# Two convolutions in a transformed form and mixer attention in groups of four heads, in an eight-image stack on one core

## The chip, the core and the metric

The kernel runs on one core of a Trainium2 chip. Five engines work side by side, each with its own queue in order: TensorE (PE; its weight loads are listed as PEld), VectorE (DVE), ScalarE (ACT), GpSimd (POOL) and SyncE (SP), which here issues most DMAs. The metric is device time in microseconds, the median of the runs.

## The reference

Input `x` is 8 images of 256 channels on 32 x 32 pixels, in fp32. Four layers follow, each adding to `x` what it makes of its group norm (`_gn`, 32 groups). Cut to what matters here:

```
x = x + attention(gn(x))       # 8 heads of 64, l2-normed q and k, scale 10, 1024 tokens
x = x + conv3x3(gn(x), scaling_factors * quant_weights) + bias
x = x + conv3x3(gn(x), kernel) + bias
x = x + mixer(gn(x))           # per-token norm, 4 selective scans of 1024 steps, gates,
                               # depthwise and pointwise convolutions, 8-head attention
                               # with heads of 32 over 1024 tokens, gelu, 3x3 depthwise, projection
```

Both convolutions have 256 channels in and out, padding 1. The attention of the mixer is

```
att = softmax(q @ k.transpose(0, 1, 3, 2) * (1.0 / hd ** 0.5), axis=-1)     # hd = 32, 8 heads
o = (att @ v).transpose(0, 2, 1, 3).reshape(B, N, Cc)
```

## The kernel before, in words

A channel tile is 128 channels on the 128 partitions, so an image is two tiles of 1024 pixels. Each image goes through the stages A (`front_attention`), O (`front_out`), C (`front_convs`), N and S (`scan_layers`, `scan_steps`), B (`back_layers`, with `mixer_attention`) and E (`back_out`, `back_end`). The engine calls are not issued as they stand: `Plan` records them, and `arrange` orders them for all eight images together, engine by engine, with costs, buffer rooms and due marks (`PACE`) that are written in the file. So stages of different images lie beside each other, in an order that is fixed when the kernel is built. All recorded operations carry one line of the file (L238), so instructions are told apart by their tiles.

PSUM has five rooms: `big` (two tiles of 1024 columns, two banks each), and one bank each of `acc`, `cv`, `da` and `y`. An fp32 product is two TensorE records, a weight load and a matmul each.

A convolution (`conv3x3`) writes the normed image into two padded buffers `im` (34 x 34). For each output tile m and image half h it adds 18 products (two input tiles, nine taps), each of 128 weights columns and 512 pixels, in the one bank `cv`; the weights come as chunks `w` by DMA from ACT's queue, three taps each; then one DVE operation adds the bank to `xt`.

In `mixer_attention` a head has 32 rows. A query tile exists twice, `q[0]` and `q[1]`, each with every other head zeroed (`alt`), so that a product over 64 rows holds one head of two. A unit of `attention` is a pair of heads, a half of the queries and one of eight key tiles: two products of 64 rows side by side (rows 0 to 63 and 64 to 127) fill one `big` tile, ACT takes its exponential (`p<-big`), and two products of 128 x 64 side by side add the values into `acc` (32 value columns and 32 columns of ones per head, the latter for the sums). Values are two units behind scores. `front_attention` has the same form with heads of 64 (`big<-q,k`), and DVE adds up its `p`.

A scan step works on 128 x 1024 elements: POOL multiplies (`hs<-du,bc`), ACT makes two decays (`da`), DVE scans twice, POOL multiplies again (`hs<-hs,bc`); two steps are added up by four products of 32 columns side by side in the bank `y`, 32 such y sums per image. It is fed by DMAs (`du`, `dt`, `bc`) on SP's queue.

Of the kernel before, what the change touches and what calls it, by code (L numbers as in the profile page):

```python
# [2 lines left out]

# [8 lines left out]
F32 = mybir.dt.float32  # L12
I32 = mybir.dt.int32
AF = mybir.ActivationFunctionType
ALU = mybir.AluOpType
# [10 lines left out]
TW = 34 * 34  # L26
# [8 lines left out]
STAGGER = {(128, 128): 5, (64, 128): 109, (128, 64): 56, (128, 32): 29, (32, 128): 150}  # L35
# [3 lines left out]
        (1090, 1090, 1090, 1090),  # L39
        (1794, 2079, 2159, 2247),  # L40
        (3309, 3371, 3408, 3447),
        (4080, 4158, 4180, 4325),
        (4886, 4936, 4988, 5063),
        (5486, 5486, 5525, 5567),
        (6054, 6187, 6240, 6330),
        (7000, 7131, 7262, 7440),
    ),
    "B": (
        (3642, 3818, 3933, 4116),
        (4392, 4437, 4642, 4768),  # L50
        (5155, 5196, 5269, 5284),
        (5865, 5879, 5885, 5955),
        (6550, 6707, 6766, 6867),
        (7291, 7976, 8075, 8299),
        (8403, 8480, 8525, 8749),
        (9837, 9880, 9886, 10001),
    ),
    "C": (
        (2076, 2079, 2141, 2145),
        (2646, 2654, 3354, 3704),  # L60
        (3701, 3911, 4065, 4167),
        (4759, 4784, 4869, 5136),
        (5163, 5377, 5466, 5761),
        (5860, 5879, 6054, 6514),
        (6799, 6868, 6880, 6904),
        (7491, 7558, 7582, 7829),
    ),
    "E": (
        (4096, 4096, 4186, 4285),
        (4827, 4899, 5232, 5286),  # L70
        (5329, 5699, 5832, 6106),
        (6092, 6263, 6350, 7109),
        (7060, 7136, 7688, 7737),
        (8379, 8504, 8574, 8868),
        (9303, 9830, 9895, 10037),
        (12374, 12684, 12908, 13007),
    ),
    "F0": (
        (500, 1149, 1149, 1149),
        (-298, -204, 165, 223),  # L80
        (856, 856, 1011, 1234),
        (2412, 2540, 2540, 2545),
        (-8734, -8678, -8368, -8368),
        (2539, 2864, 4457, 4747),
        (1390, 1390, 1513, 1727),
        (4562, 4572, 4578, 4668),
    ),
    "F1": (
        (2106, 2111, 2131, 2179),
        (1796, 1796, 1943, 2563),  # L90
        (3041, 3041, 3062, 3385),
        (4004, 4068, 4068, 4079),
        (1464, 1603, 1608, 1661),
        (2220, 2318, 2708, 2708),
        (6533, 6538, 6538, 6538),
        (6838, 6870, 6870, 6870),
    ),
    "F2": (
        (2557, 2557, 2685, 3068),
        (3542, 3875, 3875, 3945),  # L100
        (4588, 4595, 4629, 4796),
        (5254, 5343, 5412, 5494),
        (5461, 5871, 5969, 5969),
        (6121, 6642, 6800, 6815),
        (5287, 5445, 5473, 5473),
        (8235, 8306, 8489, 8489),
    ),
    "F3": (
        (3180, 3225, 3267, 3267),
        (3890, 3973, 4076, 4076),  # L110
        (4837, 4838, 4839, 4875),
        (5365, 5369, 5608, 5614),
        (6028, 6083, 6190, 6253),
        (6951, 6955, 6958, 7027),
        (7760, 7854, 8086, 8143),
        (4383, 4745, 5335, 5637),
    ),
    "N": (
        (516, 521, 576, 640),
        (1685, 1687, 2171, 2279),  # L120
        (3467, 4308, 4335, 4362),
        (4483, 4935, 5214, 5225),
        (722, 722, 722, 722),
        (5342, 5342, 5750, 5750),
        (6697, 7072, 7477, 7666),
        (8019, 8302, 8375, 8470),
    ),
    "O": (
        (1416, 1416, 1461, 1501),
        (2356, 2398, 2577, 3153),  # L130
        (3472, 3472, 3472, 3767),
        (4390, 4412, 4416, 4632),
        (5158, 5187, 5225, 5247),
        (5567, 5729, 5751, 5753),
        (6353, 6426, 6427, 6427),
        (7469, 7505, 7506, 7745),
    ),
    "S": (
        (-2043, -509, -169, -165),
        (3552, 3950, 4007, 4072),  # L140
        (4424, 4639, 4959, 5095),
        (3087, 3087, 3087, 3599),
        (-925, -925, -925, -920),
        (3181, 3197, 3203, 3218),
        (3306, 3356, 3356, 3362),
        (7486, 8460, 8543, 8559),
    ),
    "Z0": (
        (2489, 2516, 2580, 2586),
        (-3362, -2551, -2535, -2535),  # L150
        (931, 956, 959, 993),
        (5172, 5207, 5244, 5272),
        (5898, 5898, 5898, 5969),
        (5487, 5487, 5633, 6007),
        (4040, 4070, 4451, 4451),
        (4234, 4308, 4510, 4518),
    ),
    "Z1": (
        (2722, 2752, 3010, 3024),
        (3910, 4021, 4027, 4328),  # L160
        (4647, 4710, 4751, 5149),
        (5328, 5336, 5340, 5374),
        (6040, 6055, 6055, 6115),
        (6520, 6662, 6676, 6688),
        (7664, 7763, 7994, 8414),
        (529, 1313, 1832, 1833),
    ),
    "Z2": (
        (2447, 3260, 3700, 3822),
        (4280, 4280, 4288, 4288),  # L170
        (4852, 4940, 4994, 4994),
        (5570, 5570, 5750, 5886),
        (5953, 6085, 6229, 6295),
        (7061, 7127, 7200, 7329),
        (8177, 8177, 8357, 8478),
        (9006, 9173, 9266, 9274),
    ),
# [1972 lines left out]
```

## Time and profile before

| | us |
|---|---|
| median of 3 runs | 5774.64 (5768.99 to 5777.19) |
| profiled run, its own time | 5783.67 |
| span of the profile | 5781.9, granted TensorE clock 0.941 |
| busy: PE, DVE, ACT, POOL | 5224.1, 3673.7, 2694.6, 2610.2 |
| PE on convolutions, 2304 records | 1076.8 |
| PE on mixer scores (`qk`), 2048 records | 583.1 |
| PE on values of both attentions, 4096 records | 1104.5 |
| PE on front scores (`q,k`), 2048 records | 585.2 |
| ACT on exponentials, 1024 | 1037.4 |
| DVE adding convolution banks to `xt`, 32 and 32 | 23.6 and 21.6 |

A busy time is that of one profiled execution. Groups of PE overlap each other a little, as matmuls are pipelined, and the mean of one matmul includes its latency. Idle time before a group is put down to what released it. Where a row counts records, two make one product.

### The profile page before, as it was taken

How to read it: one execution, taken by the hardware profiler on the slowest of the kernel's cores; microseconds unless marked ns; L12 is line 12 of the kernel's file. 1: busy time of each engine (PE TensorE's matmuls, PEld its weight loads, DVE VectorE, ACT ScalarE, POOL GpSimd, SP SyncE). 2: the span in 40 equal slices, each digit the busy share in tenths (PEclk: the TensorE clock that was granted, in tenths of full speed). 3: DMA queues.
4: the chain of work that ended last, by engine and by line, in shares of the span. 5: the costliest groups of instructions: out<-in, count | busy, mean ns of one | idle time of the engine just before them, and what ended most of it. 6: DMA issues, size and time to landing. Idle time of an engine off the chain costs nothing.

```text
span 5781.9 us, 52549 instructions
## 1 busy us (share of the span) xinstructions
PE 5224.1 (90%) x17318; PEld 1811.6 (31%) x17318; DVE 3673.7 (64%) x4517; ACT 2694.6 (47%) x3115; POOL 2610.2 (45%) x1302
## 2 busy tenths in 40 slices
PE   8999789999999989999899999998989988868895
PEld 3333232332333233333323323342233332322333
DVE  4434757666776668646678647866466665677713
ACT  3323334545454544545454554544635436546442
POOL 0000865178601864118533745509650377497500
PEclk9999789999999989999999999999999999879897
DMA  1112433144402433124422433224340354233200
GB/s 52 31 49 82 129 109 106 54 122 124 128 24 80 126 108 94 46 59 136 119 76 66 133 96 110 79 67 134 93 134 17 110 148 114 83 106 106 74 21 32
DMA packets 252411, 516.99 MB, mean 89 GB/s; under 512 B 65112, under 2 KB 131288, under 8 KB 252128
## 3 DMA queue, kind: packets, MB, share of 16 engines
q1 hardware_dynamic: 168032, 402.35, 24.8%
q10 hardware_dynamic: 84096, 111.19, 6.8%
q8 instruction: 139, 2.28, 0.2%
q14 instruction: 144, 1.18, 0.1%
HBM read 448.84 MB, written 56.10 MB: 87 GB/s over the span
## 4 chain that ended last, share of the span: by engine, by line
PE 37%; DVE 12%; DMA 6%; ACT 4%; POOL 3%; issue 3%; SPq 0%; ACTq 0%; DVEq 0%; POOLq 0%
PE big L238 21%; PE acc L238 8%; PE cv L238 6%; DVE hs L238 4%; POOL hs L238 3%; PE y L238 2%; ACT da L238 2%; DVE room L238 2%; DMA dt<-dt_m 1%; DVE u L238 1%; DMA du_m<-a 1%; DMA w<-in_wc 1%; DVE p L238 1%; DMA dt_m<-dt 1%; ACT p L238 1%
## 5 line engine op out<-in xcount | busy, mean ns | idle before, releaser
L238 POOL TENSOR_TENSOR hs<-du,bc 128x1024 f32<-128x1024 f32 x512 | 1245.7, 2440 | 2529.3 <-DMA du<-du_m 1813.2
L238 ACT ACTIVATE p<-big 128x1024 f32<-128x1024 f32 x1024 | 1037.4, 1020 | 807.9 <-PE big L238 732.4
L238 POOL TENSOR_TENSOR hs<-hs,bc 128x1024 f32<-128x1024 f32 x512 | 1295.3, 2531 | 187.5 <-DVE hs L238 115.6
L238 ACT ACTIVATE da<-dt,a_neg 128x512 f32<-128x512 f32 x1024 | 707.2, 691 | 1135.1 <-DVE hs L238 894.1
L238 PE MATMUL cv<-im,w 128*128 128x512 f32 x2304 | 1076.8, 614 | 54.0 <-ACT im L238 21.0
L238 PE MATMUL acc<-p,v 128*64 128x512 f32 x4096 | 1104.5, 623 | 8.5 <-ACT both L238 3.0
L238 DVE TENSOR_TENSOR_SCAN hs<-da,hs 128x512 f32<-128x512 f32 x512 | 624.5, 1220 | 404.9 <-ACT da L238 268.1
L238 DVE TENSOR_TENSOR_SCAN hs<-da,carry,hs 128x512 f32<-128x512 f32 x512 | 654.9, 1279 | 338.8 <-ACT da L238 269.1
L238 DVE TENSOR_TENSOR p<-p 128x1024 f32<-128x1024 f32 x448 | 600.0, 1340 | 275.9 <-ACT p L238 210.5
L238 PEld LDWEIGHTS cv<-im,w 128*128 128x128 f32 x2304 | 429.8, 194 | 681.8 <-issue 562.8
L238 PE MATMUL big<-qk,qk 64*128 64x512 f32 x2048 | 583.1, 650 | 63.4 <-ACT p L238 37.3
L238 PE MATMUL big<-q,k 64*128 64x512 f32 x2048 | 585.2, 652 | 58.7 <-ACT k L238 20.6
L238 PEld LDWEIGHTS acc<-p,v 128*64 128x64 f32 x4096 | 214.8, 136 | 775.1 <-issue 691.6
L238 PE MATMUL y<-hs,sel 128*32 128x512 f32 x2048 | 338.6, 643 | 85.5 <-POOL hs L238 83.7
L238 PEld LDWEIGHTS big<-qk,qk 64*128 64x128 f32 x2048 | 160.7, 188 | 473.4 <-issue 231.0
L238 PEld LDWEIGHTS big<-q,k 64*128 64x128 f32 x2048 | 160.7, 189 | 466.8 <-issue 256.0
L238 PE MATMUL big<-xn,w 128*128 128x512 f32 x512 | 231.9, 603 | 7.2 <-ACT big L238 3.5
L238 PE MATMUL big<-o,w 128*128 128x512 f32 x384 | 178.7, 608 | 8.2 <-DVE o L238 7.0
L238 DVE SCALAR_TENSOR_TENSOR room<-room,vec,room 128x992 f32<-128x992 f32 (+1 forms) x128 | 160.7, 1255 | 9.7 <-ACT room L238 8.1
L238 DVE SCALAR_TENSOR_TENSOR u<-raw,vec,u 128x1024 f32<-128x1024 f32 x96 | 141.8, 1477 | 31.1 <-ACT u L238 30.2
L238 PE MATMUL big<-xm,w_minw 64*128 64x512 f32 x256 | 137.0, 651 | 18.9 <-DVE room L238 6.5
L238 PEld LDWEIGHTS y<-hs,sel 128*32 128x32 f32 x2048 | 49.2, 110 | 321.5 <-POOL hs L238 187.9
(220 smaller groups left out, 4845.6 us busy)
## 6 DMA issues: line engine op xcount, KB each, us to landing
bc<-bc SPq DMA_DIRECT2D x1024, 128.0 KB
w<-in_wc ACTq DMA_DIRECT2D x384, 192.0 KB
dt<-dt_m SPq DMA_DIRECT2D x512, 128.0 KB
du<-du_m SPq DMA_DIRECT2D x512, 128.0 KB
rs<-inv SPq DMA_DIRECT2D x64, 256.0 KB
dt_m<-dt SPq DMA_DIRECT2D x64, 256.0 KB
du_m<-a SPq DMA_DIRECT2D x64, 256.0 KB
w<-in_wqk ACTq DMA_DIRECT2D x64, 128.0 KB
```

The costliest lines, as they stand in the source:

```text
L238: made = op["call"](*args, **kwargs).ins
```

## The change

It has three parts. **Convolutions.** Two neighbouring pixels of a row are made of four products instead of six: the normed image is split into odd and even columns and turned into four tap images (`taps`: a difference, a sum, a difference and a difference), each 16 columns wide, in halves of 16 rows with their border rows (`transform`, on ACT and DVE). For each output tile and image half, 24 products of 256 pixels (four taps, three rows, two input tiles) go in two turns of 12 through the bank `cv`; `add_products` adds the first turn to `xt` with three DVE operations and the second with one. The weights of the inner taps are half sums and half differences of the three weights of a row; `conv_weights` makes them once, at the start, and writes all to DRAM (stage V). A chunk `w` is now 256 KB, of four matrices.

**Scores.** `q` is no longer zeroed by heads, and four products of 32 rows, one for each head of a tile, fill both `big` tiles; two exponentials follow. **Values.** The four heads of a unit go to two banks, `acc` for two heads and `cv` for the other two, one unit behind the scores. The number of exponentials and of value products is as before.

The planner learns of it: products of 32 rows may be grouped over two tiles, a group may take several buffers at once, PE's writes count as whole banks, and the due marks of all stages and one charge for product shapes (`STAGGER`) are other numbers. The diff, without the due marks, the planner's bookkeeping, and the copying out of values, which stays in kind:

```diff
-STAGGER = {(128, 128): 5, (64, 128): 109, (128, 64): 56, (128, 32): 29, (32, 128): 150}
+STAGGER = {(128, 128): 5, (64, 128): 109, (128, 64): 56, (128, 32): 29, (32, 128): 300}
...
+def whole_banks(r):
+    return r[:3] + (r[3] // HALF * HALF, r[4] // HALF * HALF + HALF - 1)
...
-                if joins and first.tensor.name == out.tensor.name:
+                beside = first.tensor.name == out.tensor.name or rows == 32
+                if joins and beside:
...
+        if op["engine"] == 0:
+            outs = [whole_banks(r) for r in outs]
...
-        src = fc_w if name == "fcw" else I[name]
+        src = made_w.get(name, I[name])
...
+    made_w = {"fcw": fc_w}
+    for name in ("wc1", "wc2"):
+        made_w[name] = wdp.tile([12, P, 4, P], F32, tag=name, name=name)
+    minus_s1 = wp.tile([P, 2], F32, name="minus_s1")
+    vector.tensor_scalar_mul(minus_s1, vec[:, cols["s1"] : cols["s1"] + 2], -1.0)
...
-    images = [wp.tile([P, TW], F32, name="im%d" % t) for t in range(2)]
+    taps = wp.tile([P, 2, 4, 18, 16], F32, name="taps")
...
-    def conv3x3(xt, mv, made, name, bname, evac):
-        im = [t.rearrange("p (h w) -> p h w", w=34) for t in images]
-        group_norm(
-            xt, group_stats(mv, cv_tile), [t[:, 1:33, 1:33] for t in im], image
-        )
-        for m in range(2):
-            scalar.activation(xt[m], xt[m], AF.Identity, bias=col(bname, m))
-        for m in range(2):
-            for h in range(2):
-                ps = cv_tile()
-                n = 0
-                for c in range(2):
-                    for dy in range(3):
-                        w = chunk(name, (m * 2 + c) * 3 + dy)
-                        for dx in range(3):
+    def conv_weights(name):
+        for i in range(6):
+            w = room[0][:, 0 : 6 * P].rearrange("p (c k n) -> p c k n", c=2, k=3)
+            sync.dma_start(out=w, in_=I[name][i])
+            sums = room[1][:, 0 : 4 * P].rearrange("p (c k n) -> p c k n", c=2, k=2)
+            plus, minus = sums[:, :, 0], sums[:, :, 1]
+            vector.tensor_add(plus, w[:, :, 0], w[:, :, 2])
+            vector.tensor_scalar_mul(w[:, :, 1], w[:, :, 1], 0.5)
+            vector.scalar_tensor_tensor(
+                minus, plus, 0.5, w[:, :, 1], ALU.mult, ALU.subtract
+            )
+            vector.scalar_tensor_tensor(
+                plus, plus, 0.5, w[:, :, 1], ALU.mult, ALU.add
+            )
+            inner_w, outer_w = (
+                made_w[name][2 * i + k].rearrange("p (c k) n -> p c k n", c=2)
+                for k in range(2)
+            )
+            sync.dma_start(out=inner_w, in_=sums)
+            for k in range(2):
+                sync.dma_start(out=outer_w[:, :, k], in_=w[:, :, 2 * k])
+    def transform(xt, stats, h):
+        scale, shift = stats
+        rows = slice(0, 17) if h == 0 else slice(16, 32)
+        n = rows.stop - rows.start
+        if h == 0:
+            vector.memset(taps[:, :, :, 0], 0.0)
+        else:
+            vector.tensor_copy(taps[:, :, :, 0], taps[:, :, :, 16])
+            vector.memset(taps[:, :, :, 17], 0.0)
+        for c in range(2):
+            t = taps[:, c, :, 1 : 1 + n]
+            for k, at in ((1, 1), (2, 0)):
+                scalar.activation(
+                    t[:, k],
+                    image(xt[c])[:, rows, at:32:2],
+                    AF.Identity,
+                    bias=shift[:, c : c + 1],
+                    scale=scale[:, c : c + 1],
+                )
+            odd, even = t[:, 1], t[:, 2]
+            vector.tensor_sub(t[:, 0, :, 1:16], odd[:, :, 0:15], odd[:, :, 1:16])
+            vector.tensor_sub(t[:, 3, :, 0:15], even[:, :, 1:16], even[:, :, 0:15])
+            for k, src, at in ((0, odd, 0), (3, even, 15)):
+                scalar.mul(t[:, k, :, at], src[:, :, at], -1.0)
+            vector.tensor_add(odd, odd, even)
+            vector.scalar_tensor_tensor(even, even, -2.0, odd, ALU.mult, ALU.add)
+    def add_products(x, ps, inner_taps, scales):
+        pixels = x.rearrange("p (h w k) -> p k h w", w=16, k=2)
+        products = ps.rearrange("p (k h w) -> p k h w", k=2, w=16)
+        def add(to, part, scale, minus=False):
+            if scale is not None:
+                vector.scalar_tensor_tensor(to, part, scale, to, ALU.mult, ALU.add)
+            else:
+                (vector.tensor_sub if minus else vector.tensor_add)(to, to, part)
+        plus, minus = scales or (None, None)
+        if inner_taps:
+            shape = [P, 2, 16, 16]
+            add(pixels, products[:, 0].unsqueeze(1).to_broadcast(shape), plus)
+            add(pixels[:, 0], products[:, 1], plus)
+            add(pixels[:, 1], products[:, 1], minus, True)
+        else:
+            add(pixels, products, plus)
+    def conv3x3(xt, mv, made, name, bname, scales, finish):
+        stats = group_stats(mv, cv_tile)
+        for h in range(2):
+            half = HALVES[h]
+            transform(xt, stats, h)
+            for m in range(2):
+                scalar.activation(
+                    xt[m][:, half], xt[m][:, half], AF.Identity, bias=col(bname, m)
+                )
+            for m in range(2):
+                for part, ks in enumerate(((1, 2), (0, 3))):
+                    ps = cv_tile()
+                    w = [chunk(name, (m * 3 + dy) * 2 + part) for dy in range(3)]
+                    for i, k in enumerate(ks):
+                        for n in range(6):
+                            dy, c = divmod(n, 2)
                             tensor.matmul(
-                                image(ps),
-                                w[:, dx],
-                                im[c][:, 16 * h + dy : 16 * h + dy + 16, dx : dx + 32],
+                                ps[:, i * C : (i + 1) * C].rearrange(
+                                    "p (h w) -> p h w", w=16
+                                ),
+                                w[dy][:, 2 * c + i],
+                                taps[:, c, k, dy : dy + 16],
                                 start=n == 0,
-                                stop=n == 17,
+                                stop=n == 5,
                             )
-                            n += 1
-                evac(m, HALVES[h], ps)
+                    add_products(xt[m][:, half], ps, part == 0, scales(m))
                 if h == 1:
                     channel_stats(made, m, xt[m])
+                finish(m, half)
...
         xt = img.pop("x")
-        def evac_1(m, part, ps):
-            part = xt[m][:, part]
-            vector.scalar_tensor_tensor(
-                part, ps, col("s1", m), part, ALU.mult, ALU.add
-            )
+        def scales(m):
+            return col("s1", m), minus_s1[:, m : m + 1]
         mv = stats_tile()
-        conv3x3(xt, img.pop("mv"), mv, "wc1", "b1", evac_1)
+        conv3x3(xt, img.pop("mv"), mv, "wc1", "b1", scales, lambda m, half: None)
         img["xd"] = xdp.tile([P, 2, N], F32, tag="xd", name="xd")
-        def evac_2(m, part, ps):
-            vector.tensor_add(xt[m][:, part], xt[m][:, part], ps)
-            sync.dma_start(out=img["xd"][:, m, part], in_=xt[m][:, part])
-        conv3x3(xt, mv, mvs[:, img["at"]], "wc2", "b2", evac_2)
+        def finish(m, half):
+            sync.dma_start(out=img["xd"][:, m, half], in_=xt[m][:, half])
+        conv3x3(
+            xt, mv, mvs[:, img["at"]], "wc2", "b2", lambda m: None, finish
+        )
         img["made"] = True
...
                             stop=c == 1,
                         )
                 if at == t:
-                    q = [work("qk3")[:, 0:N] for _ in range(2)]
+                    q = work("qk3")[:, 0:N]
                     vector.tensor_scalar(
-                        q[0], ps, col("ain_b", t), alt[:, 0:1], ALU.add, ALU.mult
-                    )
-                    scalar.activation(
-                        q[1], ps, AF.Identity, bias=alt_b[:, t, 1:2], scale=alt[:, 1:2]
+                        q, ps, col("ain_b", t), 32.0**-0.5, ALU.add, ALU.mult
                     )
                 else:
                     k = work("qk3")[:, 0:N]
...
-        attention([lambda i=i: pair(i) for i in (0, 1, 4, 5)], False)
+        def scores(u):
+            if u["t"] not in qk:
+                q_and_k(u["t"])
+            (q, k), kt = qk[u["t"]], u["kt"]
+            s = [big_tile() for _ in range(2)]
+            for e in range(4):
+                rows = slice(e * 32, e * 32 + 32)
+                tensor.matmul(
+                    s[e // 2][:, HALVES[e % 2]],
+                    k[rows, kt * P : (kt + 1) * P],
+                    q[rows, HALVES[u["h"]]],
+                    start=True,
+                    stop=True,
+                )
+            u["p"] = [work("p")[:, 0:N] for _ in range(2)]
+            for p, ps in zip(u["p"], s):
+                scalar.activation(p, ps, AF.Exp)
+        def values(u):
+            t, h, kt = u["t"], u["h"], u["kt"]
+            if kt == 0:
+                accs[t, h] = acc_tile(), cv_tile()
+            for at, acc in enumerate(accs[t, h]):
+                for e in range(2):
+                    tensor.matmul(
+                        acc[e * 64 : e * 64 + 64],
+                        v[:, kt, 4 * t + 2 * at + e],
+                        u["p"][at][:, HALVES[e]],
+                        start=kt == 0,
+                        stop=kt == NKT - 1,
+                    )
+            if kt == NKT - 1:
+                take(t, h)
...
+        sums, accs = {}, {}
+        units = [
+            {"t": t, "h": h, "kt": kt}
+            for t in range(2)
+            for h in range(2)
+            for kt in range(NKT)
+        ]
+        for n in range(len(units) + 1):
+            for stage, at in ((scores, n), (values, n - 1)):
+                if 0 <= at < len(units):
+                    stage(units[at])
...
+    with plan.part("V", 0):
+        conv_weights("wc1")
+        conv_weights("wc2")
...
-        return c(w.transpose(0, 2, 4, 3, 5, 1).reshape(12, P, 3, P))
+        return c(w.transpose(0, 4, 3, 2, 5, 1).reshape(6, P, 2, 3, P))
```

## The prediction

> **What bounds the kernel now.** I read the page first: the shares of the engines and the row of the granted clock.
>
> ```profile
> PE 5224.1 (90%) x17318; PEld 1811.6 (31%) x17318; DVE 3673.7 (64%) x4517; ACT 2694.6 (47%) x3115; POOL 2610.2 (45%) x1302
> ...
> PEclk9999789999999989999999999999999999879897
> ```
>
> TensorE is busy nine tenths of the span; the others have room on average. An average hides stages, so I cut the span where the PE order gives a landmark. The orders of the two kernels show that everything issued on PE before the first y sum of image 6's scan is the same work in both, convolutions apart; that sum starts at 4596 us. Columns: stretch, length, busy time of PE, PEld, DVE, ACT, POOL, granted clock, DMA share, GB/s.
>
> ```profile
> 0.00:4596.00 4596.00, 4257.97 (x14036) 1472.54 (x14036) 2966.88 (x3769) 2147.25 (x2490) 1978.92 (x991) 0.96 0.32 90
> 4596.00:5010.00 414.00, 371.37 (x1257) 128.38 (x1256) 267.23 (x277) 204.56 (x245) 304.78 (x152) 0.94 0.43 119
> 5010.00:5432.00 422.00, 317.44 (x1084) 98.25 (x1084) 322.72 (x281) 218.38 (x260) 325.64 (x160) 0.84 0.39 109
> 5432.00:5782.00 350.00, 277.32 (x947) 112.41 (x946) 116.84 (x191) 124.37 (x120) 0.90 (x1) 0.85 0.08 24
> 2200.00:2300.00 100.00, 99.23 (x325) 31.19 (x325) 85.55 (x104) 48.52 (x59) 49.43 (x26) 1.00 0.30 84
> ```
>
> To 4596 us PE is 93% busy: less PE work is time there. In the third stretch, the last scan, PE is 75% busy and POOL has 326 us of 422: the scan sets the pace. The last is image 7's back half, a chain. The fifth row shows that DVE at 85% does not slow PE.
>
> Next the groups of instructions, shapes apart (count | busy us, mean ns | idle before it and its releasers).
>
> ```profile
> L238 PE MATMUL cv<-im,w 128*128 128x512 f32 x2304 | 1076.8, 614 | 54.0 <-ACT im L238 21.0 <-DMA w<-in_wc 18.6 <-DVE xt L238 14.3
> L238 ACT ACTIVATE p<-big 128x1024 f32<-128x1024 f32 x1024 | 1037.4, 1020 | 807.9 <-PE big L238 732.4 <-PE cv L238 14.1 <-DVE t L238 8.5
> ...
> L238 PE MATMUL big<-qk,qk 64*128 64x512 f32 x2048 | 583.1, 650 | 63.4 <-ACT p L238 37.3 <-DVE a L238 10.4 <-DVE qk L238 10.1
> ```
>
> A product is two records, so 1152 convolution products and 512 pairs of mixer scores. PE waits little for either: 54 and 63 us.
>
> **Convolutions.** 18 products of 512 columns per (m, h) become 24 of 256. The 256-column shape is already there, in the values of the mixer; the timeline has two runs of it.
>
> ```profile
> 1204.05 3.72 PE L238 MATMUL big<-w,x 128*128 128x256 f32 x16
> ...
> 2485.99 7.17 PE L238 MATMUL big<-w,x 128*128 128x256 f32 x32
> ```
>
> (7.17 - 3.72)/16 = 0.216 us a record. Rows of 512 columns (16 records 7.03 us, 8 records 3.60 us) give 0.429, so the shape halves cleanly, and a weight load of 0.19 us still fits under 0.216. By the orders, 1044 of 1152 products lie before the landmark now, and 1476 of 1536 after the change: 2088 x 0.429 = 896 us against 2952 x 0.216 = 638. That is 258 us at full clock, 269 at the 0.96 granted. The Trainium skill (TensorEngine Tiling (Array Packing), Instruction Overhead) speaks against many short products: some 60 cycles are lost on each. Read as an addition at the 2.4 GHz of its page TensorE: Matmul & The Clock Gate, the 864 more records would cost an estimated 22 us and the gain would be 247; the row shows none of it, and the measurement decides.
>
> What convolutions gain in hand-overs: one PSUM bank (cv) now turns 128 times instead of 64, and the tap buffer is filled 32 times instead of 16. Now a turn costs PE 14.3/64 = 0.22 us and a fill 21.0/16 = 1.3; at these prices +14 and +21, so +35 us. Lower bound 0. The upper bound is a turn with nothing on PE to cover it; that is a rival below. In the order most turns have scores, values or y sums between (one run of 42 products has none).
>
> DVE: from 512-column rows (0.738 scaled, 0.676 plain) and 1024-column rows (1.273, 1.209) an operation is 0.14 to 0.20 us plus 1.04 ns a column. A filled half image is four operations of about 0.44 us on each channel tile: 64 x 1.74 = 111 us. An evacuation pair is 2.4 or 2.2 us, 64 of them 147 us, against 45 now. With small copies 10 and the weight transform 20, DVE gets 243 us more, 3917 in all, 73% of 5400. I cost it at nothing, since the last windows row above runs PE at 99% beside 85% DVE; if that cover fails it is part of the third rival. ACT: identities on 272 columns instead of 1024, about +70 us, less 19 for the second scaled copy of q that goes: under 1% of the span, cost 0. DMA: chunks of 256 instead of 192 KB, 25 MB more; weights cost PE 18.6 us now and twelve short products need 768 KB in 5.2 us, so 0 to 25 us; I take 0, since runs are spread among attention.
>
> The weight transform puts 48 DMAs on SP's queue and 48 DVE operations into the first 280 us, ahead of sums, few, inv and rs of image 0's attention. DVE is half idle there and the first convolution starts near 280 us; twelve rounds of load, four operations and stores at some 8 us (estimate) are 96 us. Cost 0, at most 30 if the stores hold up the normalisers.
>
> **Mixer scores.** Now a pair of 64-row products, an exp, a pair of values:
>
> ```profile
> 4100.78 1.13 PE L238 MATMUL big<-qk,qk 64*128 64x512 f32 x4
> ...
> 4101.84 1.08 PE L238 MATMUL acc<-p,v 128*64 128x512 f32 x4
> ...
> 4102.02 1.03 ACT L238 ACTIVATE p<-big 128x1024 f32<-128x1024 f32 x1 [1.04 <-PE big L238]
> 4102.85 0.30 PEld L238 LDWEIGHTS big<-qk,qk 64*128 64x128 f32 x4 [0.81 <-issue]
> ```
>
> One round takes 4102.85 - 4100.78 = 2.07 us, PE without a gap, ACT idle half of it. Two rounds, four heads: 4.14. After it: one quad of 32-row products, two exps, two pairs of values. No row here has 32-row products. Nearest: the y sums, four 32-column products side by side, 1.06 us; and the pair, whose four loads take 0.30 (0.19 + 3 x 0.037), so eight take 0.45 and the quad 1.06 + 0.15 = 1.21. Other end: two pairs one after the other, 2.12, or four single products, 3.45. I take 1.21, because both packed forms in the trace do overlap.
>
> PE then needs 1.21 + 2 x 0.99 = 3.19. But a quad fills both big buffers, so the next quad waits for both exps: 1.24 from quad to first exp (4102.02 - 4100.78), 2 x 1.03, and some 0.15 back (that first exp starts 0.11 after its pair's 1.13), 3.45 us. That chain, not PE, sets the round: 0.69 saved instead of 0.95. In ACT's order 49 of 256 quads have another operation between their exps, nearly always a decay (0.69 us); 36 are in images 0 to 5. Other ACT work has the 1.24 us. Before the landmark: 160 quads x 0.69 less 36 x 0.69 = 85 us, 89 at clock 0.96. Queued behind a quad waiting on PE are values and y sums, and so the scan; a y sum stands in every third round and fits its gap. The skill's PSUM Bottleneck section (same Tiling page) warns that packed products move the limit to the engine that empties PSUM. The trace has that engine 0.26 us per round behind PE, which is the chain just priced; were ACT always late by a decay, the round would be 4.1 and this term about 0.
>
> **Sum**, from the span of 5781.9:
> - to the landmark 4596 - 269 - 89 + 35 = 4273;
> - scan of image 6: 414 loses nearly all its convolution and a third of its scores, but POOL alone has 305 and the last scan, with PE free, took 422: 395;
> - scan of image 7, already paced by the scan: 415;
> - image 7's back half: 350 - 32 x 0.69 = 328.
>
> Together 5411, with 1.8 us around the span 5413. The profiled run (5783.7) is 9 above the median (5774.6), so 5404; I say 5400, 6.5% less.
>
> **Rivals.**
> 1. The covers hold better: quads at PE's 3.19 with decays in the gaps (-70), turns hidden (-35), two scans nearer to POOL's 320 (-45): 5250. For it: PE at 97 to 99% in busy windows. Against: both big buffers are taken by one quad.
> 2. The change does not do what it says: 32-row products run two abreast. The round is 2.12 + 1.98 = 4.1 as now, so 89 + 22 come back: 5510. Four in a row, 5.43 a round: 160 x 1.29/0.96 + 89 before the landmark and 63 in the back half, 5770. For: no such row. Against: y's quads at 1.06.
> 3. DVE is late now and then: a quarter of the hand-overs below stand uncovered: 5520.
> 4. Slower: the one cv bank and the one tap buffer. A turn without cover is an evacuation of 1.7, a scan of 1.2 ahead of it on DVE and 0.3 of signalling, 3.2 us; 128 are 410. A fill is four ACT and eight DVE operations, about 6 us; 32 are 190. All uncovered: 5400 - 35 + 600 = 5965; at three quarters 5815. It decides from 68%, where 5775 is reached. For: one bank, in-order queues. Against: 0.22 us a turn today.
>
> **How the numbers follow.** Forecast 5400 (own range 5310 to 5480) 0.55; rival 1 0.20; rival 2 0.09; rival 3 0.11; rival 4 0.05. The range 5220 to 5540 takes in rivals 1 to 3, and leaves out part of rival 1, four-in-a-row quads and rival 4. The three runs spread by 0.14%; about 0.2% is what can be told from no change. Faster 0.94, same 0.01, slower 0.05.
>
> **What would show it.** Right: cv records near 0.22 us apart and PE's cv group near 700 us; a qk quad near 1.2 us; ACT's two exps back to back and PE idle about 0.3 us a round, put down to ACT p; idle before cv below 120 us; DVE about 3900 us; the two last scans still about 400 us each. Wrong: quads over 2 us (rival 2), cv idle of 200 us or more released by DVE xt or ACT taps (rivals 3 and 4), or first y sum of image 6 later than 4400 us.

## The result, and the profile after

The changed kernel takes **5817.3 us** (median of 5 runs) where the kernel before takes 5774.6. The ratio of the two kernels is 1.0077, 95% interval 1.0057 to 1.0098: slower by 0.8%. I had forecast 5400.

First the page of the changed kernel: busy times and their share of the span, then the granted clock in 40 slices.

```profile
PE 4872.9 (84%) x18086; PEld 1946.9 (33%) x18086; DVE 3930.9 (68%) x5060; ACT 2709.1 (47%) x3353; POOL 2611.0 (45%) x1295
...
PEclk9999889888998889989899989989999877888796
```

PE's busy time fell by 351 us, but its idle time rose from 5781.9 - 5224.1 = 558 to 5815.6 - 4872.9 = 943. The second row is why the busy time fell by so little: the mean granted clock went from 0.941 to 0.896. In both traces the clock is granted either whole or half; PE was busy for 467 us at half clock before and for 799 after. Counting these at half, I estimate PE's work at full clock as 4991 us before and 4473 after. So some 518 us of PE work did go; about 167 came back as a lower clock, and 385 as idle time.

The stretches of the prediction, cut at the same landmark (the first y sum of image 6, now at 4613.4). Columns as there: stretch, length, busy PE, PEld, DVE, ACT, POOL, clock, DMA share, GB/s.

```profile
0.00:4613.40 4613.40, 3996.64 (x14908) 1633.42 (x14908) 3222.44 (x4319) 2175.20 (x2729) 1987.66 (x988) 0.92 0.35 99
```

Up to the landmark I had 4273; it is 4613, against 4596 before. Most of the error, 340 of some 404 us, is in this one stretch: PE is 87% busy in it instead of 93%, at a clock of 0.92 instead of 0.96. From the landmark to the end of the last y sum of image 7 it is 875 us where it was 838 and where I had 810. Image 7's back half alone came out as forecast: 328 us, from 5488 to the end.

PE's waits, longest sums first (us, times, longest); first before, then after.

```profile
PE y L238 <- POOL hs L238: 83.7, 37, 5.8
PE big L238 <- ACT p L238: 59.6, 45, 10.1
```

```profile
PE y L251 <- POOL hs L251: 199.2, 82, 12.2
PE acc L251 <- ACT p L251: 133.3, 147, 9.6
PE big L251 <- DVE u L251: 49.1, 12, 12.8
```

PE now comes to a y sum 82 times before POOL has weighed the scan's states, and to the values 147 times before ACT has made the exponentials. Most of both lies where scans run. I added up PE's idle time by slices of 100 us: in slices where POOL, which works for the scans, is at least 40% busy it rose from 326 to 642 us, elsewhere from 232 to 300. One pair of such slices, before and then after (columns: slice, length, busy PE, PEld, DVE, ACT, POOL, clock, DMA share, GB/s):

```profile
4700.00:4800.00 100.00, 96.68 (x310) 36.89 (x310) 68.72 (x60) 43.16 (x55) 83.67 (x42) 0.98 0.58 159
```

```profile
4700.00:4800.00 100.00, 55.03 (x144) 17.73 (x144) 71.21 (x57) 31.80 (x40) 70.55 (x35) 0.68 0.33 87
```

PE falls from 97 to 55% and its clock from 0.98 to 0.68, while DVE and POOL, at 71% each, are the busiest and neither is near full. So the busy time of no single engine accounts for that slice.

The pieces themselves are as I sized them. Two runs of convolution products in the timeline (start, us, engine, instruction):

```profile
935.25 5.45 PE L251 MATMUL cv<-taps,w 128*128 128x256 f32 x24
965.41 1.56 PE L251 MATMUL cv<-taps,w 128*128 128x256 f32 x6
```

(5.45 - 1.56)/18 = 0.216 us a record, the value of the sum (the whole group is 762.6 us busy, where I had said near 700). And image 7's mixer, which has no scan beside it:

```profile
5578.62 1.08 PE L251 MATMUL cv<-p,v 128*64 128x512 f32 x4
5578.78 1.94 ACT L251 ACTIVATE p<-big 128x1024 f32<-128x1024 f32 x2 [1.38 <-PE big L251]
5579.86 1.08 PE L251 MATMUL acc<-p,v 128*64 128x512 f32 x4 [0.16 <-ACT p L251]
5580.87 1.14 PE L251 MATMUL big<-qk,qk 32*128 32x512 f32 x8
5581.94 1.08 PE L251 MATMUL cv<-p,v 128*64 128x512 f32 x4
5582.10 1.94 ACT L251 ACTIVATE p<-big 128x1024 f32<-128x1024 f32 x2 [1.38 <-PE big L251]
```

A round is 5582.10 - 5578.78 = 3.32 us, where I had 3.45. The quad takes 5581.94 - 5580.87 = 1.07, where a pair of 64-row products took 1.06 before: four products of 32 rows do run side by side.

### The profile page after: what moved, and what is told of

Read it like the earlier page. It is cut to its first block, busy times and chain, and to the rows that moved or that the text cites. A ratio compares the mean times of both kernels' runs of the same rounds, so it can differ in the third digit from the quotient of the medians.

```text
span 5815.6 us, 55053 instructions
## 1 busy us (share of the span) xinstructions
PE 4872.9 (84%) x18086; PEld 1946.9 (33%) x18086; DVE 3930.9 (68%) x5060; ACT 2709.1 (47%) x3353; POOL 2611.0 (45%) x1295
## 4 chain that ended last, share of the span: by engine, by line
PE 49%; DVE 19%; DMA 10%; ACT 8%; POOL 7%; issue 5%; SPq 1%; ACTq 0%; DVEq 0%; POOLq 0%
PE big L251 27%; PE acc L251 9%; PE cv L251 9%; POOL hs L251 7%; DVE hs L251 6%; ACT p L251 3%; DMA dt_m<-dt 2%; ACT da L251 2%; PE y L251 2%; DMA dt<-dt_m 2%; DVE p L251 2%; SPq L251 1%; DVE u L251 1%; DVE room L251 1%; DMA du<-du_m 1%
## 5 line engine op out<-in xcount | busy, mean ns | idle before, releaser
L251 ACT ACTIVATE p<-big 128x1024 f32<-128x1024 f32 x1024 | 1018.4, 1019 | 670.0 <-PE big L251 582.5
L251 PE MATMUL acc<-p,v 128*64 128x512 f32 x3072 | 854.1, 640 | 141.5 <-ACT p L251 133.3
L251 PE MATMUL cv<-taps,w 128*128 128x256 f32 x3072 | 762.6, 402 | 105.3 <-DVE taps L251 35.4
L251 PEld LDWEIGHTS cv<-taps,w 128*128 128x128 f32 x3072 | 597.7, 200 | 346.8 <-issue 136.6
L251 PE MATMUL y<-hs,sel 128*32 128x512 f32 x2048 | 413.3, 689 | 206.4 <-POOL hs L251 199.2
L251 PEld LDWEIGHTS acc<-p,v 128*64 128x64 f32 x3072 | 164.9, 139 | 744.3 <-issue 373.3
L251 PE MATMUL big<-qk,qk 32*128 32x512 f32 x2048 | 369.1, 697 | 46.2 <-ACT raw L251 14.0
L251 PE MATMUL cv<-p,v 128*64 128x512 f32 x1024 | 288.1, 636 | 2.7 <-DVE xt L251 2.7
L251 PEld LDWEIGHTS big<-qk,qk 32*128 32x128 f32 x2048 | 101.9, 198 | 299.8 <-issue 196.4
L251 POOL COPY carry<-hs 128x2 f32<-128x2 f32 x256 | 107.4, 420 | 169.1 <-DVE hs L251 145.6
```

Of the source, the lines that this page charges most:

```text
L251: made = op["call"](*args, **kwargs).ins
```

## The experiments

Theories after the first look: **A**, the quads lock PE to ACT and the scan; **B**, the convolutions' new work on DVE and their single bank eat the gain; **C**, the order, which the planner makes from costs and due marks, decides, whatever the work is. Times are medians; ratios stand against runs of the kernel before that were made beside each.

### One part alone, a control, and the old marks

The first two kernels are the changed one with one part put back; the third is the program of before under the planner of the change; the fourth is the changed one with the marks of before.

```diff
 # e1: conv3x3, transform, add_products, conv_weights of the change
-        ... (scores and values in units of four heads)
+        attention([lambda i=i: pair(i) for i in (0, 1, 4, 5)], False)
 # e2: units of four heads
-    def conv3x3(xt, mv, made, name, bname, scales, finish):
+    def conv3x3(xt, mv, made, name, bname, evac):
 # e4
-PACE = {"A": ((-805, -722, -708, -698), ...
+PACE = {"A": ((1090, 1090, 1090, 1090), ...
```

> The convolutions of the change alone (four products per two pixels, tap buffer, weight transform), with the mixer attention of before; planner of the change, marks of before. Theory A (the quads lock the mixer to ACT and the scan; the convolutions keep their gain): about 269 - 35 us less than before, 5500 to 5580 us. Theory B (the convolutions' DVE work, which waits on POOL, and the single cv bank eat their gain): 5750 us or more. Theory C (the order of the planner, not the work, makes the difference): anything, but as far from before as the control with the program of before under the same planner is.

> The mixer attention of the change alone (quads of 32-row scores, values in two banks), with the convolutions of before; planner of the change, marks of before. Theory A: no gain or a loss, 5770 to 5950 us, and PE waits for ACT p ahead of acc for 100 us or more. Theory B: the gain that I predicted for the scores, some 110 us, stays: 5640 to 5700 us. Theory C: as far from before as the control.

> Control: the program of before, with its marks, ordered by the planner of the change (which counts a PSUM write as a whole bank, gives out several tiles at once and costs 32-row products at more). Theories A and B: within 0.5% of before, 5746 to 5803 us. Theory C: over 1% from before, so that a comparison of single parts must allow for that much.

> The changed program with the due marks of before (the weight transform keeps its own). Theory C (the new marks are what costs the time): 5400 to 5600 us. Theories A and B (the work itself sets the time): 5800 us or more, the marks of the change fitting it better than those of before.

| | us | ratio to before (95%) |
|---|---|---|
| e1, convolutions alone, marks of before | 6209.5 | 1.0787 (1.0755 to 1.0819) |
| e2, quads alone, marks of before | 6448.5 | 1.1188 (1.1165 to 1.1210) |
| e3, program and marks of before, new planner | 5768.7 | 1.0000 (0.9987 to 1.0012) |
| e4, change with marks of before | 6375.5 | 1.1061 (1.1036 to 1.1085) |

e2 missed every forecast. e1 lies in B's range (5750 or more) and e4 in that of A and B (5800 or more), but both are so far beyond what the change itself costs that this speaks for neither. The planner's edits are neutral for the program of before (e3). A program that is ordered by marks made for another is 8 to 12% slower here, ten times or more what the change costs. So single parts can't be judged in such an order, and A and B stay open here. Each of the three shows the same wait first among PE's (e2, then e4; 341.5 us in e1):

```profile
PE y L242 <- POOL hs L242: 486.6, 164, 11.6
```

```profile
PE y L241 <- POOL hs L241: 509.6, 171, 10.9
```

The marks say when the work of each stage and image is due, and so where it stands in the orders of the engines. In these three orders PE meets the scan's y sums too early: this wait was 83.7 us before.

### Less work in the same order

To test the work without the order, I left products out after the order had been made: every engine keeps its list, and only the named instructions are missing. These programs, and e10 and e12 below, leave out a part of the result and serve to price work alone. In e7 one memset of the tap buffer at the start is added.

```diff
-        for n in arrange(self.ops, self.rooms):
+        for n in (k for k in arrange(self.ops, self.rooms) if not self.ops[k].get("left_out")):
...
 # e5, in the kernel before, after each product
+                            plan.ops[-1]["left_out"] = plan.recording and dx == 1
 # e6, in the changed kernel, after each product
+                            plan.ops[-1]["left_out"] = plan.recording and n in (1, 3)
 # e7: in transform, each of the four DVE operations after the two activations
```

> The kernel before, every engine's instructions in the same order, but the convolutions' products with the middle column of taps (dx = 1) left out: 384 of 1152 products, 768 records x 0.429 = 330 us of PE work, as much as the change takes off the convolutions, and nothing added. Step on test: 'to 4596 us PE is 93% busy: less PE work is time there'. If it holds: 0.9 x 330 = 300 us less, 5450 to 5500 us. If it fails (the orders of ACT, DVE and POOL are as long as PE's, and PE only fills their waits with convolutions): under 80 us less, 5690 to 5775 us; PE idle grows by about what its busy time loses, the granted clock falls, and PE's wait for POOL hs ahead of y grows.

> The changed kernel, every engine's instructions in the same order, but a third of the convolutions' products left out (the second channel tile in two of three rows of taps): 512 of 1536 products, 1024 records x 0.216 = 221 us of PE work. If PE's work sets the time after the change: about 190 us less, near 5630 us. If the other engines' orders do: within 60 us of the changed kernel, 5755 to 5820 us.

> The changed kernel, every engine's instructions in the same order, but DVE's four operations that make the transformed taps left out in all fills (256 operations, some 120 us of DVE with their waits on POOL). If DVE's new work, or its turns with POOL, is what delays the scan and with it PE (the cover that I costed at nothing): 100 us or more less, 5715 us or below. If the orders set the pace and DVE has room: within 40 us of the changed kernel, 5775 to 5855 us, a little of either sign.

e5 took 5712.9 us, ratio 0.9900 (0.9884 to 0.9917): 330 us of PE work less, nothing added, and 55 us gained on the runs of before made beside it. The page and PE's first waits of e5:

```profile
PE 4992.5 (87%) x16550; PEld 1680.8 (29%) x16550; DVE 3679.7 (64%) x4517; ACT 2693.3 (47%) x3115; POOL 2608.4 (46%) x1302
...
PE 48%; DVE 21%; DMA 11%; POOL 7%; ACT 7%; issue 6%; SPq 1%; ACTq 0%; DVEq 0%; POOLq 0%
PE big L238 29%; PE acc L238 11%; DVE hs L238 8%; POOL hs L238 6%; PE cv L238 5%; ACT da L238 3%; DMA dt<-dt_m 2%; PE y L238 2%; DMA w<-in_wc 2%; DVE p L238 2%; DVE room L238 2%; DMA dt_m<-dt 2%; DVE u L238 2%; SPq L238 1%; ACT p L238 1%
```

```profile
PE y L238 <- POOL hs L238: 115.3, 60, 6.4
PE big L238 <- ACT p L238: 77.3, 56, 10.1
PE cv L238 <- DVE xt L238: 51.8, 20, 9.1
```

PE's busy time falls by 232 us and its idle time rises from 558 to 724; the clock goes from 0.941 to 0.926. The second part of the page is the chain that ended last: though PE is busy 87% of the span, it holds 48% of the chain, and `cv` only 5%. By this chain, convolutions mostly fill PE's time while other work holds the end.

e6 took 5749.7 us, 68 below the changed kernel's 5817.3, for 221 us of PE work: just beyond the bound of 60 that I had set for orders, and far from 190. e7 took 5768.8 us, 48 below it: between my two cases. 256 DVE operations took 3930.9 - 3783.9 = 147 us, 0.57 each where I had 0.44. Three quarters of them in the changed kernel (count; min, median and max in ns; first and last start in us; shapes):

```profile
L251 DVE TENSOR_TENSOR taps<-taps x192: 376/418/2609, 241.1 to 4633.2; 128x255 f32<-128x255 f32 x64, 128x240 f32<-128x240 f32 x64, 128x272 f32<-128x272 f32 x32, 128x256 f32<-128x256 f32 x32
```

Most take 0.42 us, but some 2.6; POOL's multiplications take 2.4 to 2.5. One place in the timeline of the changed kernel, DVE and POOL alone:

```profile
822.76 0.43 DVE L251 SCALAR_TENSOR_TENSOR taps<-taps 128x272 f32<-128x272 f32 x1
822.94 7.50 POOL L251 TENSOR_TENSOR hs<-du,bc 128x1024 f32<-128x1024 f32 x3 [31.68 <-DMA du<-du_m]
823.11 5.11 DVE L251 TENSOR_TENSOR taps<-taps 128x255 f32<-128x255 f32 x2
828.33 2.41 DVE L251 SCALAR_TENSOR_TENSOR taps<-taps 128x272 f32<-128x272 f32 x1
```

While POOL multiplies three times, three operations on the taps take 2.4 to 2.6 us each. Over the whole trace 34 of the 256 take more than 0.7 us, 72 us together. In each of the 34 a POOL instruction was already running when the operation started, and 32 of them ended 0.26 to 0.30 us after that instruction did; of the 221 that took at most 0.5 us only 18 overlap POOL at all. So these operations wait for POOL. The Trainium skill (SBUF — State Buffer, Who interferes with whom) says that DVE's second pair of SBUF ports is GpSimd's too, under an exclusive lock; the trace agrees with it. Cover that I had priced at nothing cost up to 48 us in this order; it is a part, not the cause.

### Less work in an order made anew

```diff
 # e10 and e12, in the kernel before
                         for dx in range(3):
+                            if dx == 1:
+                                n += 1
+                                continue
 # e8, e9, e11 to e14: other numbers in PACE alone
```

For new marks I varied them step by step and kept what the planner reckoned to end no later; e8 and e9 for about as long as each other, e11 to e14 longer.

> The changed kernel with other due marks: the same instructions, the marks varied step by step and kept wherever the planner's own reckoning ended no later, some hundred thousand steps from the marks of the change. If the order alone holds back what PE was spared: far below both, 5400 to 5600 us. If the new marks only trim an order that is as long in the other engines as in PE: 1 to 2% below the changed kernel, 5700 to 5770 us, and no further below the next run than the changed kernel is from the one before.

> The control to the last run: the kernel before with marks varied in the same way and for as long from its own. If the marks of before were closer to their best than those of the change (the change was only less well ordered): within 0.3% of before, 5750 to 5785 us. If both were as far from it: 1 to 1.5% below, 5690 to 5720 us, and still no slower than the changed kernel with new marks.

> As the second run before these (the kernel before without the convolutions' products of the middle column of taps, 330 us of PE work less), but here the planner never sees those products and makes its order anew, with the marks of before. If less PE work is worth time in any sensible order: at most the 5713 us of the run in the old order. If the marks fit one program's work and no other: slower than before though it does less, 5850 to 6000 us, with PE waiting for POOL hs ahead of y for 200 us or more.

> The changed kernel with marks varied for longer, from those of its first run with new marks (5762 us). If that was still badly ordered: 5720 to 5745 us, 0.4 to 0.8% under the kernel before. If 5762 us was about what this program can do: 5750 to 5770 us. In neither case do I now expect the 5400 us of my forecast.

> The kernel before without the convolutions' products of the middle column of taps (330 us of PE work less; planned without them, as in the run that took 5984 us), with marks varied for this program. Compare with the kernel before with new marks, 5733 us. If an order made for it turns PE work into time: 300 us less than that, near 5430 us. If the other engines' orders are nearly as long as PE's however it is ordered: 60 to 140 us less, 5590 to 5675 us, a fifth to two fifths of the work.

> The convolutions of the change alone, as in the run of 6209 us, with marks varied for this program. If the 6209 us were the order: 5720 to 5800 us, within 1.2% of the kernel before with new marks (5733 us). If the convolutions themselves are slow (DVE's taps, the single bank): 5850 us or more. My own sum would have it 235 us below 5733.

> The mixer attention of the change alone, as in the run of 6448 us, with marks varied for this program. If the 6448 us were the order: 5740 to 5840 us. If the quads themselves are slow beside a scan (both big tiles taken, exps behind decays): 5900 us or more. My own sum would have it 110 us below 5733.

| | us | ratio to before (95%) | PE idle | clock |
|---|---|---|---|---|
| e8, change, new marks | 5761.6 | 0.9987 (0.9969 to 1.0006) | 905 | 0.900 |
| e9, before, new marks | 5733.5 | 0.9944 (0.9925 to 0.9964) | 508 | 0.942 |
| e10, before less a third of the products, marks of before | 5984.3 | 1.0382 (1.0359 to 1.0405) | 904 | 0.898 |
| e11, change, marks varied for longer | 5695.8 | 0.9878 (0.9861 to 0.9894) | 862 | 0.903 |
| e12, as e10, new marks | 5618.6 | 0.9750 (0.9734 to 0.9766) | 646 | 0.926 |
| e13, convolutions alone, new marks | 5760.7 | 0.9984 (0.9972 to 0.9997) | 751 | 0.916 |
| e14, quads alone, new marks | 5729.9 | 0.9948 (0.9930 to 0.9966) | 661 | 0.929 |

(PE idle is the span less PE's busy time of the profiled run; e5 is the run that e10's text means.)

e10 does less than the kernel before and is 219 us slower. Its first wait of PE:

```profile
PE y L238 <- POOL hs L238: 336.9, 119, 10.4
```

It was 83.7 us before. The same products in the old order took 5712.9 (e5), so what made e10 slow is the order. With marks of its own (e12) the same program takes 5618.6, which is 115 below e9, for 330 us of PE work. So an order made for the lighter program turns about a third of the work into time, and less if the longer search for e12's marks gave a part of it; in the old order it was a sixth. In e12 PE holds 55% of the chain:

```profile
PE 4960.9 (88%) x16550; PEld 1674.3 (30%) x16550; DVE 3681.7 (66%) x4517; ACT 2688.8 (48%) x3113; POOL 2600.4 (46%) x1302
...
PE 55%; DVE 18%; DMA 10%; ACT 7%; POOL 5%; issue 4%; SPq 1%; ACTq 0%; DVEq 0%; POOLq 0%
```

e13 and e14 show that the 6209 and 6448 us of e1 and e2 were mostly the order: in orders of their own the parts take 5761 and 5730, e13 within my bounds and e14 a little below them. Neither is clearly better than e9, though their marks were varied for longer, so neither part alone brought what I had summed for it (235 and 110 us below e9).

e12 and e13 together say more. By the estimate used above for the kernels before and after, their PE work at full clock is the same, 4670 and 4680 us; both were ordered anew, and e13 takes 142 us more. What the convolutions of the change add beside their products (251 us of DVE work, hand-overs, larger weight chunks, the weight transform) took back all that the lighter products gained; my sum had it at 35. So theory B holds for the convolutions, as far as two orders can be compared. e7's 48 us for four of DVE's operations, in another order, is the only piece of it that was priced. For the quads, e14's values wait 92.0 us for ACT p, where e9 has 10.7 us of idle time before values in all: that fits theory A, and no run takes the wait away.

e11, the changed kernel, is 121 us faster than with the marks that it came with, below the 5720 that I gave as the lowest, and 1.2% faster than before: the version that beats both. Its page and waits:

```profile
PE 4838.9 (85%) x18086; PEld 1938.7 (34%) x18086; DVE 3920.1 (69%) x5060; ACT 2703.0 (47%) x3353; POOL 2602.6 (46%) x1295
```

```profile
PE y L241 <- POOL hs L241: 167.3, 67, 10.7
PE acc L241 <- ACT p L241: 146.8, 141, 9.9
```

The wait for POOL hs shrank from 199 to 167 us; the wait of values for ACT p did not, and PE still idles 862 us. e9 missed both of its cases: 0.6% better than before, so the marks of before were closer to good ones than those of the change, but not at their best. e8 against e9, varied alike, is 5761.6/5733.5 = 1.005, so the change did not gain in that comparison. e11 against e9 is 5695.8/5733.5 = 0.993, but its marks were varied for longer.

**Open.** A control for e11, the kernel before with marks varied as long, was not run; the gain of the change at equal care of the order lies, by e8, e9 and e11, between a loss of 0.5% and a gain of 0.7%, and a better order may exist for any of them. Which of the other engines holds the rest is not separated either: PE waits for the scan on POOL and for exponentials on ACT in every run. No run here has POOL's or ACT's work taken away.

## Why the prediction was wrong

The step that failed is the one behind every term up to the landmark: **"To 4596 us PE is 93% busy: less PE work is time there."** e5 tests it without the change: 330 us of PE work are worth 55 us, a sixth, where the step gives 300, and e12 at most 115 in an order made for it. The first y sum of image 6 then started at 4613, past the 4400 that I had named as a sign of being wrong. A busy share says what an engine does, not what the end waits for. The page of before had rows against it, which I did not weigh: its chain that ended last.

```profile
PE 37%; DVE 12%; DMA 6%; ACT 4%; POOL 3%; issue 3%; SPq 0%; ACTq 0%; DVEq 0%; POOLq 0%
PE big L238 21%; PE acc L238 8%; PE cv L238 6%; DVE hs L238 4%; POOL hs L238 3%; PE y L238 2%; ACT da L238 2%; DVE room L238 2%; DMA dt<-dt_m 1%; DVE u L238 1%; DMA du_m<-a 1%; DMA w<-in_wc 1%; DVE p L238 1%; DMA dt_m<-dt 1%; ACT p L238 1%
```

The shares add up to 65%, for the chain is followed back only to 1940 us. PE holds 37 of the 65, and `cv` 6 of the 65, about a tenth, where convolutions are a fifth of PE's busy time (1076.8 of 5224.1). If the first third is like the rest, a third of the convolutions is then worth 0.06/0.65/3 = 3% of the span, an estimate of some 178 us, if nothing else came late next; 55 were measured. So the chain warns, and it still priced the work too high.

Two rows of the changed kernel for what follows: a wait of PE up to the landmark (us, times, longest), and the group of convolution products (busy us, mean ns | idle before).

```profile
PE acc L251 <- ACT p L251: 94.0, 85, 9.6
```

```profile
L251 PE MATMUL cv<-taps,w 128*128 128x256 f32 x3072 | 762.6, 402 | 105.3 <-DVE taps L251 35.4
```

By the terms of the sum:
- **Convolutions, 269.** The size was right (0.216 us a record). Its worth was not: 55 us for as much work in the old order (e5), at most 115 in an order of its own (e12), and nothing once the work that comes with it is there (e13).
- **Scores, 89.** The quad (1.07 against 1.21) and the round without a scan (3.32 against 3.45) were right, and the back half of image 7 came out at 328 as said. The wait for ACT was near its price too. The sum allows 0.26 us in each of 160 rounds up to the landmark and a decay in 36 rounds, some 66 us; there the changed kernel has, front attention included, 94.0. What the sum put at nothing is the y sum, which "fits its gap": up to the landmark PE's wait for POOL hs rose from 41.7 to 116.9 us. And the PE work that was saved was not time: the quads alone, in an order of their own (e14), are 4 us below e9, where the sum has 110.
- **Hand-overs, 35.** Idle before convolution products rose from 54.0 to 105.3 us, by 51: near the 35, and below my mark of 120. Rival 4 priced this at 600. That it has 5815 at three quarters, and 5817 was measured, is luck: PE does not wait that long for the bank and the tap buffer.
- **DVE at nothing.** It came to 3930.9 us against 3917 foretold. The cover did not hold wholly: e7 gives up to 48 us for the taps, with operations that wait for POOL, and e13 against e12 gives 142 us for all that the convolutions add.
- **Clock.** I divided by the clock of before, 0.96, as if it were given. It fell to 0.92 in that stretch. The traces show what goes ahead of a drop: in the 3.4 us before the clock falls to half, PE was busy 40% of the time in the kernel before and 34% in the changed one, against 90 and 84% over the span. At half clock a convolution record takes 0.427 us instead of 0.216. So work that is taken off PE and leaves gaps lowers the clock for a part of what remains; e5 shows it with nothing added (0.941 to 0.926).
- **The two last scans.** I left them near their length, but on the wrong side: 838 became 875 us together, not 810.

Rival 2 falls by the quads. Of the Trainium skill's two rules (both on its page TensorEngine Tiling (Array Packing)), Instruction Overhead, read as an addition, cost nothing seen at 256 columns: 0.216 us a record is half of the 0.429 at 512. PSUM Bottleneck, which says that emptying PSUM may set the limit after packing, agrees with the trace in kind. The whole idle time before values of `acc` was 8.5 us and is now 141.5, of which 133.3 wait for ACT p.

A case that none of my rivals held: PE's work goes down as summed and the end does not follow, because less PE work is time only in part, a sixth in the old order and a third at most in a new one. What holds the end in its place, in the orders of the other engines, stays open.

## What to carry to other kernels

A busy share of 93% doesn't make an engine's work the time: ask the chain that ended last how much of it runs through the rows that the change touches (here it still gave 178 us where 55 were measured). If a kernel can be ordered the same with some work left out, that run prices the work at once. Where a planner orders all engines from tuned marks, a changed program under old or less well tuned marks can lose more (here up to 12%) than the change can bring; compare programs only after each has had the same care of its order. And when the clock drops after gaps on PE, it takes back a part of a PE saving that leaves gaps: here some 167 of 518 us.

## What the hardware showed that I had not expected

- The granted clock fell with PE's busy share in every lighter kernel: 0.926 with a third of the convolutions gone in the old order, 0.896 with the change, and 0.68 in the slice where PE was busy 55%. It is either whole or half, and it fell to half after some 3.4 us in which PE was busy 34 to 40% on average.
- DVE operations of 0.42 us between SBUF tiles took up to 2.6 us when a POOL instruction was already running: 34 of 256, of which 32 ended 0.26 to 0.30 us after it. The mean over all 256 was 0.57.
